# Float32 tables and row-half counts in the subset look-up of a four-layer graph network

## The chip, the cores and the metric

The kernel runs on one core of one Trainium2 chip. The metric is the device time of one execution in microseconds (us), lower is better. Before the change the median of three runs is 6579.31 us, and the three lie between 6573.1 and 6581.36 us.

## The reference, cut to what matters

Sixteen graphs of N = 1024 nodes with 128 features pass four layers, each followed by a residual and a normalisation. The adjacency matrix of a graph holds only zeros and ones. The change touches layer 1 alone:

```
p = x @ (W1 - W2);  q = x @ W2
pre[i, j] = p[i] + q[j] + b
x1[i] = max over j of relu(pre[i, j]) * adj[i, j]
```

As relu is monotone, this is `relu(p[i] + b + max of q[j] over the neighbours j of i)`. The costly part is the maximum over neighbours, for 1024 nodes, 1024 possible neighbours and 128 features in each of 16 graphs.

The other layers matter as work that runs beside it: layer 0 is masked attention, layer 2 a two-layer perceptron on summed neighbours, and layer 3 three graph convolutions on a thinned ("dilated") adjacency matrix, which is found by a sequential pass over its rows.

## The kernel before, in words

**The maximum as a table look-up.** The 1024 possible neighbours of a graph are cut into `NP` = 86 groups of 12, and a group into two subgroups of `GS` = 6. A subgroup has 64 subsets, and for each subset the maximum of q over it is worked out once: two subgroups give a table of 128 rows. For a node i, the part of its adjacency row that falls on a subgroup names one subset. So the maximum over a subgroup is one row of the table, and a matrix product of the table with a one-hot column picks it out.

**One slot** handles one group s of one graph b; there are 16 x 86 = 1376 slots, and each has two halves h of 512 nodes (`halves[h]`). The loop `slot(s, last)` writes out the order of the instructions of TensorE (PE), ScalarE (ACT), VectorE (DVE) and GpSimd (POOL) by hand, and each of these engines runs its list in that order. In a half stand, in this order:

1. `look_up(s, h, pg)` (L779): four products on TensorE. A product uses 64 of the 128 rows, since a subgroup's table has 64 rows: rows 0 to 63 for subgroup a = 0, rows 64 to 127 for a = 1, into two banks of the PSUM tile `pg` (two buffers of two banks). The table is held in two pieces, `high` and `low`, both of type float32r, whose products add up in PSUM.
2. `advance(...)`: pieces of the other work, taken from generators called streams (`scores`, `attend`, `rest`, `tables_of`) by a planner that gives each engine so many microseconds of other work in each slot (`ROOM`). At a due time it also takes a piece of `dilation()`, the sequential pass for layer 3, whose chain runs on GpSimd and VectorE.
3. `low_part(s + 1)` in the first half of odd slots (L768, L770): TensorE subtracts `high` from the table in PSUM by a product with `less` (minus the identity), and ScalarE copies the rest out as `low`.
4. `count(s + 2, h)` (L748, L749): one product of the constant `lit` (plus and minus ones) with the adjacency columns `AT`, 120 rows in fp8, counts for each of the 128 subsets how well each node matches it; ScalarE then forms `relu(count + one_less)`, which is the one-hot `hot`. It runs two slots ahead of the look-up.
5. `table(s + 2)` in the second half of even slots (L760, L763): TensorE transposes two groups' subset maxima `sub` into the tile `pt`, and ScalarE copies that out as `high`.
6. VectorE takes the running maximum `best = max(best, pg)` over both subgroups, 1024 values in each partition (L831).

The tiles `pm` of `count` and `pt` of `table` share a tag, "subset", of two one-bank buffers in PSUM; `pt` is kept until `low_part` is done. The adjacency columns come by `load_columns` (L700), one DMA on GpSimd's queue for 120 rows (ten slots), two loads ahead, in four buffers.

When the slots are done, the graph convolutions of layer 3 follow in a stage of their own, which has none of this code.

Of the kernel before, what the change touches and what calls it, by code (L numbers as in the profile page):

```python
# [39 lines left out]
B, N, D, H2 = 16, 1024, 128, 256  # L40
P = 128
T = N // P
GS = 6
PS = 2 * GS
PC = 10
CH = PC * PS
NP = -(-N // PS)
TG = 12
R, G = 32, 4
# [9 lines left out]
def subset_tables():  # L59

    half = P // 2
    s = np.arange(half)
    lit = np.zeros((CH, PC, P), np.float32)
    for j in range(CH):
        a, k = divmod(j % PS, GS)
        lit[j, j // PS, a * half:(a + 1) * half] = np.where((s >> k) & 1, 1.0, -1.0)
    size = sum((s >> k) & 1 for k in range(GS))
    return lit, np.tile(1.0 - size, 2).astype(np.float32).reshape(P, 1)


@with_exitstack
def tile_graph_layers(ctx: ExitStack, tc, a, out):
    nc = tc.nc
    x, adj, adjT = a["x"], a["adj"], a["adjT"]
    halves = (slice(0, 512), slice(512, 1024))

    consts = ctx.enter_context(tc.tile_pool(name="consts", bufs=1))
    dram = ctx.enter_context(tc.tile_pool(name="dram", bufs=1, space=DRAM))
    small = ctx.enter_context(tc.tile_pool(name="small", bufs=3))
    psum = None  # L80
# [9 lines left out]
    psum = setup.enter_context(tc.tile_pool(name="psum0", bufs=2, space=PSUM))  # L90
    ident = consts.tile([P, P], F32, name="ident")
# [13 lines left out]
    less = consts.tile([P, P], F32R, name="less")  # L105
    nc.vector.tensor_scalar_mul(less, ident, -1.0)
    one_less = consts.tile([P, 1], F32, name="one_less")
    nc.sync.dma_start(out=one_less, in_=a["one_less"])
# [52 lines left out]
    pm = bank("pm")  # L161
# [74 lines left out]
    def layers_012():  # L236
# [4 lines left out]
        apool = es.enter_context(tc.tile_pool(name="apool", bufs=1))  # L241
# [451 lines left out]
        def load_columns(at):  # L693
            b, c = divmod(at, T + 1)
            if b < B:
                rows = min(CH, N - c * CH)
                t = AT[at] = apool.tile([CH, N], F8, name="AT", bufs=4)
                if rows < CH:
                    nc.gpsimd.memset(t, 0.0)
                nc.gpsimd.dma_start(out=t[:rows], in_=adjT[b, c * CH:c * CH + rows])  # L700

        An, AT, subs, qs, ps, values, exps, bests, hots, tables = ({} for _ in range(10))
        now, taken, given, held = 0, 0, {}, {}
        pending = {}
# [33 lines left out]
                        given[held[stream]] = now + 0.5  # L738
                    pending[stream] = [next(stream, None), now]

        def count(s, h):

            b, g = divmod(s, NP)
            c, r = divmod(g, PC)
            if h == 0:
                hots[s] = w2.tile([P, N], F32R, name="hot", bufs=3)
            pm = psum.tile([P, 512], F32, tag="subset", name="pm", bufs=2)
            nc.tensor.matmul(pm, lit[:, r, :], AT[b * (T + 1) + c][:, halves[h]], start=True, stop=True)  # L748
            nc.scalar.activation(hots[s][:, halves[h]], pm, AF.Relu, bias=one_less)  # L749

        def table(s):

            b, g = divmod(s, NP)
            g0 = g - g % TG
            assert ("sub", b, g0) in happened, (s, [(x.__name__, pending[x]) for x in streams], room)
            pt = psum.tile([P, 512], F32, tag="subset", name="pt", bufs=2)[:, :2 * P]
            if g + 2 - g0 == min(TG, NP - g0):
                happened["used", b, g0] = now
            for k in range(2):
                nc.tensor.matmul(pt[:, k * P:(k + 1) * P], subs[b, g0][:, g - g0 + k, :], ident, is_transpose=True,  # L760
                                 start=(k == 0), stop=(k == 1))
            high = w2.tile([P, 2 * P], F32R, name="high", bufs=2)
            nc.scalar.copy(high, pt)  # L763
            tables[s] = pt, high

        def low_part(s):
            pt, high = tables[s]
            nc.tensor.matmul(pt, less, high, start=False, stop=True, skip_group_check=True)  # L768
            low = w2.tile([P, 2 * P], F32R, name="low", bufs=2)
            nc.scalar.copy(low, pt)  # L770
            tables[s] = high, low

        def look_up(s, h, pg):

            at = s % 2
            for k, part in enumerate(tables[s - at]):
                for a in range(2):
                    rows = slice(64 * a, 64 * a + 64)
                    nc.tensor.matmul(pg[:, a], part[rows, at * P:(at + 1) * P], hots[s][rows, halves[h]],  # L779
                                     start=(k == 0), stop=(k == 1))  # L780

        def finish(b):

# [7 lines left out]
        def slot(s, last):  # L791

            nonlocal now, due, wants_bank
            now = s
            b, g = divmod(s, NP)
            if s >= 0 and g == 0:
                finish(b)
                if b + 1 < B:
                    start(tables_of(b + 1), True)
                    load_x(b + 1)  # L800
                    start(attend(b + 1))
                    start(scores(b + 1))
                if b:
                    start(rest(b - 1))
            if s >= 0 and g % PC == 0:
                load_columns(b * (T + 1) + g // PC + 2)
            for h in range(2):
                now = s + 0.5 * h
                for e in ROOM:
                    room[e] = min(room[e] + ROOM[e] / 2, ROOM[e])  # L810
                if s >= 0:
                    pg = psum.tile([P, 2, 512], F32, tag="wide", name="pg", bufs=2)
                    look_up(s, h, pg)
                advance(("PE",))
                advance(("A", "V", "Pool"))
                if s >= 0 and due <= now and not (wants_bank and taken >= 2 and given.get(taken - 2, 1e9) > now):
                    after, cost, wants_bank = next(dilate, (B * NP, 0, False))
                    due += after
                    room["V"] -= cost
                if h == 0 and s % 2 and s + 1 < last:  # L820
                    low_part(s + 1)
                if s + 2 < last:
                    count(s + 2, h)
                    if h and s % 2 == 0:
                        table(s + 2)
                if s >= 0:
                    own = bests[b][:, :, halves[h]]
                    if g == 0:
                        nc.vector.tensor_copy(own, pg)
                    else:  # L830
                        nc.vector.tensor_max(own, own, pg)  # L831
            if s >= 0:
                hots.pop(s)
# [341 lines left out]
```

## Time and profile before

| What | Value |
|---|---|
| median of 3 runs | 6579.31 us |
| span of the profiled execution | 6568.2 us |
| the profiled execution's own time | not among the times shown; the median lies 11.1 us above its span |
| slot stage, first to last look-up | 131 to 5279 us, 5148 us, 3.74 us a slot |
| stage of layer 3 after it | 5279 to 6568 us, 1289 us |
| VectorE busy in the slot stage | 4704.24 us |
| TensorE busy in the slot stage | 4529.59 us |
| ScalarE busy in the slot stage | 3168.41 us |
| GpSimd busy in the slot stage | 3563.30 us |

The profile is of one execution. Busy time is the time in which an engine has an instruction in flight. [...]records of neighbouring matmuls overlap: what a matmul costs the engine is the distance from its start to the start of the next, where nothing else holds that up. A float32 product of TensorE has two records (two passes), a float32r product one.

### The profile page before, as it was taken

The page shows a single profiled execution, that of the slowest core. Times are in us where ns is not written, and L with a number is a line of the kernel's source. Part 1 is how long each engine was busy: PE and PEld are TensorE (multiplying, and loading weights), DVE is VectorE, ACT ScalarE, POOL GpSimd, SP SyncE. Part 2 cuts the span into 40 slices and gives each one's busy share as a digit, 9 for nine tenths or more (in the row PEclk, how much of TensorE's full clock was granted, in tenths as well). Part 3 has the DMA queues.
Part 4 walks back from the last instruction along what each step waited for, and adds up shares of the span by engine and source line. Part 5 has one row for each costly group of instructions (what it writes and reads, how often), then busy time and mean ns, then how long its engine had stood idle before and what let it go on. Part 6 is the DMA issues. An engine that isn't in the chain of part 4 may idle for free. (4 is left out here: it accounts for less than half of the span.)

```text
span 6568.2 us, 85836 instructions
## 1 busy us (share of the span) xinstructions
PE 5661.4 (86%) x27177; PEld 2873.0 (44%) x27306; DVE 5317.8 (81%) x8130; ACT 3780.8 (58%) x6665; POOL 3794.2 (58%) x11157
## 2 busy tenths in 40 slices
PE   6989898989898989899989898888888768877998
PEld 3434344444343444444444444444443335555654
DVE  3999899999899999999999999999998844444445
ACT  4656566666666666666666666666665533333755
POOL 2675767676767776767677776767676611110113
PEclk8989899999898989898989998999898878888999
DMA  5121212121212121212121212121110056564555
GB/s 38 13 28 23 31 23 36 21 28 26 28 26 29 24 30 27 27 27 28 26 27 27 30 26 33 23 31 27 27 26 12 14 80 125 110 119 106 199 170 183
DMA packets 478380, 317.00 MB, mean 48 GB/s; under 512 B 301162, under 2 KB 429668, under 8 KB 473828
## 3 DMA queue, kind: packets, MB, share of 16 engines
q0 software_dynamic: 105648, 84.20, 14.9%
q1 hardware_dynamic: 367600, 226.13, 11.9%
q8 instruction: 213, 3.49, 0.2%
q10 hardware_dynamic: 4676, 1.19, 0.1%
q14 instruction: 243, 1.99, 0.1%
HBM read 412.71 MB, written 117.18 MB: 81 GB/s over the span
## 5 line engine op out<-in xcount | busy, mean ns | idle before, releaser
L831 DVE TENSOR_TENSOR best<-best,pg 128x1024 f32<-128x1024 f32 x2720 | 3234.4, 1211 | 298.4 <-PE pg L779 289.4
L749 ACT ACTIVATE hot<-pm,one_less 128x512 fp32r<-128x512 f32 x2752 | 1882.1, 688 | 1118.0 <-PE pm L748 1107.3
L779 PE MATMUL pg<-hot,high 64*128 64x512 f32 x5504 | 1471.9, 532 | 468.0 <-DVE best L831 426.2
L779 PE MATMUL pg<-hot,low 64*128 64x512 f32 x5504 | 1166.7, 420 | 0.0
L748 PE MATMUL pm<-AT,lit 120*128 120x512 fp8e4 x2752 | 1135.9, 413 | 17.9 <-ACT hot L749 10.1
L779 PEld LDWEIGHTS pg<-hot,high 64*128 64x128 f32 x5504 | 545.7, 195 | 1271.7 <-DVE best L831 801.5
L616 POOL TENSOR_SCALAR sc<-low_counts,half_mask,rest 16x1 f32<-16x1 f32 x992 | 426.5, 430 | 403.9 <-DVE rest L603 310.1
L779 PEld LDWEIGHTS pg<-hot,low 64*128 64x128 f32 x5504 | 570.2, 204 | 0.0
L748 PEld LDWEIGHTS <-lit 120*128 120x128 fp8e4 x2752 | 273.7, 99 | 618.7 <-issue 556.1
L621 POOL TENSOR_SCALAR sc<-sc 16x1 f32<-16x1 f32 x992 | 425.5, 429 | 105.0
L770 ACT CAST low<-pt 128x256 fp32r<-128x256 f32 x688 | 255.5, 371 | 393.7 <-PE pt L768 389.3
L618 POOL TENSOR_SCALAR sc<-sc 16x1 f32<-16x1 f32 x992 | 351.6, 354 | 107.7
L980 POOL TENSOR_TENSOR length<-length,mhalf 128x8 f32<-128x8 f32 x48 | 78.9, 1644 | 572.2 <-DVE length L979 572.2
L624 POOL TENSOR_SCALAR last_rank<-V,sc 16x31 f32<-16x31 bf16 (+30 forms) x992 | 384.7, 388 | 0.0
L623 POOL TENSOR_SCALAR hit<-V,sc 16x31 bf16<-16x31 bf16 (+30 forms) x992 | 372.7, 376 | 0.0
L768 PE MATMUL pt<-high,less 128*128 128x256 f32 x688 | 300.9, 437 | 66.3 <-ACT high L763 58.7
L467 DVE TENSOR_TENSOR sub<-sub,q 128x24 f32<-128x24 f32 (+11 forms) x768 | 306.5, 400 | 24.6 <-ACT q L289 10.5
L937 ACT CAST m<-near 128x1024 fp32r<-128x1024 fp8e4 x256 | 253.4, 1044 | 113.1 <-DVE near L906 59.4
L619 POOL TENSOR_SCALAR sc<-sc 16x1 f32<-16x1 f32 x992 | 269.9, 272 | 83.4
L760 PE MATMUL pt<-ident,sub 128*128 128x128 f32 x1376 | 292.8, 297 | 24.5 <-ACT hot L749 22.0
L626 POOL TENSOR_TENSOR low_counts<-low_counts,hit 16x31 f32<-16x31 f32 (+30 forms) x992 | 264.6, 267 | 77.7
L377 PE MATMUL pav<-v,eT 128*128 128x128 f32 x2048 | 307.6, 296 | 1.9 <-ACT eT L370 1.9
(258 smaller groups left out, 9431.7 us busy)
## 6 DMA issues: line engine op xcount, KB each, us to landing
removed<-gone SPq DMA_DIRECT2D x128, 256.0 KB
An<-in_adj_dram POOLq DMA_DIRECT2D x16, 1024.0 KB, 14.8
E<-in_adj_dram POOLq DMA_DIRECT2D x128, 128.0 KB, 6.8
gone_all<-removed POOLq DMA_DIRECT2D x64, 256.0 KB, 12.1
near<-in_adjT_dram POOLq DMA_DIRECT2D x16, 1024.0 KB, 17.3
kept<-near SPq DMA_DIRECT2D x16, 1024.0 KB
share<-share SPq DMA_DIRECT2D x32, 512.0 KB
hidden<-r SPq DMA_DIRECT2D x32, 512.0 KB
```

The source lines that it names most:

```text
L377: nc.tensor.matmul(pav, eT[:, c, :], values[b][:, c, :], start=(c == 0), stop=(c == T - 1))
L467: nc.vector.tensor_max(sub[:, :n_g, n:2 * n], sub[:, :n_g, 0:n], qg[:, 2 * g0:2 * g0 + n_g, k:k + 1].to_broadcast([P, n_g, n]))
L616: gp.tensor_scalar(half, mine, half_mask[:, m], rest[:, n:n + 1], op0=ALU.mult, op1=ALU.add)
L618: gp.tensor_scalar(sf, half, 5.5, sf, op0=ALU.is_gt, op1=ALU.mult)
L621: gp.tensor_scalar(to, at, sf, none, op0=ALU.subtract, op1=ALU.subtract)
L623: gp.tensor_scalar(hit[:, n, n + 1:], V[:, n, n + 1:], at, None, op0=ALU.is_equal)
L624: gp.tensor_scalar(last[:, n + 1:], V[:, n, n + 1:], to, None, op0=ALU.is_le)
L748: nc.tensor.matmul(pm, lit[:, r, :], AT[b * (T + 1) + c][:, halves[h]], start=True, stop=True)
L749: nc.scalar.activation(hots[s][:, halves[h]], pm, AF.Relu, bias=one_less)
L768: nc.tensor.matmul(pt, less, high, start=False, stop=True, skip_group_check=True)
L779: nc.tensor.matmul(pg[:, a], part[rows, at * P:(at + 1) * P], hots[s][rows, halves[h]], start=(k == 0), stop=(k == 1))
L831: nc.vector.tensor_max(own, own, pg)
```

## The change

The table is kept in one float32 piece instead of two float32r pieces; `low_part`, `less` and the copy `low` are gone, and a look-up has two float32 products instead of four float32r ones. The counts of both node halves are made at once, in the first half of a slot: the adjacency columns lie in bf16, nodes 0 to 511 in partitions 0 to 59 and nodes 512 to 1023 in partitions 64 to 123, and a 61st row of ones (partitions 60 and 124) adds the bias that came from `one_less`. The two products of 61 rows go into the two banks of one tile `pm`, and one activation over 1024 columns makes `hot`. The tag "subset" now has one buffer of two banks, which `pm` and `pt` take in turn. The columns lie in three fixed tiles, set to one at the start, and are loaded by two DMAs (four for a graph's last, short chunk). The program has 320 such DMAs in place of 144.

```diff
-        for j in range(CH):
+        for j in range(SUB):                      # SUB = CH // 2 = 60
-    lit = consts.tile([CH, PC, P], F8, name="lit")
+    lit = consts.tile([P, PC // 2, P], BF, name="lit")
...
-                t = AT[at] = apool.tile([CH, N], F8, name="AT", bufs=4)
-                if rows < CH:
-                    nc.gpsimd.memset(t, 0.0)
-                nc.gpsimd.dma_start(out=t[:rows], in_=adjT[b, c * CH:c * CH + rows])
+                t = AT[at] = columns_in[at % len(columns_in)]
+                for part, s in enumerate(halves):
+                    whole = rows // SUB
+                    first = c * CH + whole * SUB
+                    nc.gpsimd.dma_start(out=t[64 * part:64 * part + SUB, :whole],
+                                        in_=adjT[b, c * CH:first, s].rearrange("(j r) m -> r j m", r=SUB))
+                    if rows % SUB:
+                        nc.gpsimd.dma_start(out=t[64 * part:64 * part + rows % SUB, whole],
+                                            in_=adjT[b, first:first + rows % SUB, s])
...
+        columns_in = [apool.tile([P, 2, 512], BF, name=f"AT{i}") for i in range(3)]
+        for t in columns_in:
+            nc.vector.memset(t, 1.0)
...
-        def count(s, h):
+        def count(s):
...
-            if h == 0:
-                hots[s] = w2.tile([P, N], F32R, name="hot", bufs=3)
-            pm = psum.tile([P, 512], F32, tag="subset", name="pm", bufs=2)
-            nc.tensor.matmul(pm, lit[:, r, :], AT[b * (T + 1) + c][:, halves[h]], start=True, stop=True)
-            nc.scalar.activation(hots[s][:, halves[h]], pm, AF.Relu, bias=one_less)
+            j, r = divmod(r, PC // 2)
+            hots[s] = w2.tile([P, N], F32, name="hot", bufs=3)
+            pm = psum.tile([P, 2, 512], F32, tag="subset", name="pm", bufs=1)
+            for part in range(2):
+                rows = slice(64 * part, 64 * part + SUB + 1)
+                nc.tensor.matmul(pm[:, part], lit[rows, r, :], AT[b * (T + 1) + c][rows, j, :], start=True, stop=True)
+            nc.scalar.activation(hots[s], pm.rearrange("p h n -> p (h n)"), AF.Relu)
...
-            pt = psum.tile([P, 512], F32, tag="subset", name="pt", bufs=2)[:, :2 * P]
+            pt = psum.tile([P, 2, 512], F32, tag="subset", name="pt", bufs=1)[:, 0, :2 * P]
...
-            high = w2.tile([P, 2 * P], F32R, name="high", bufs=2)
-            nc.scalar.copy(high, pt)
-            tables[s] = pt, high
-        def low_part(s):
-            pt, high = tables[s]
-            nc.tensor.matmul(pt, less, high, start=False, stop=True, skip_group_check=True)
-            low = w2.tile([P, 2 * P], F32R, name="low", bufs=2)
-            nc.scalar.copy(low, pt)
-            tables[s] = high, low
+            tables[s] = w2.tile([P, 2 * P], F32, name="table", bufs=2)
+            nc.scalar.copy(tables[s], pt)
...
-            for k, part in enumerate(tables[s - at]):
-                for a in range(2):
-                    rows = slice(64 * a, 64 * a + 64)
-                    nc.tensor.matmul(pg[:, a], part[rows, at * P:(at + 1) * P], hots[s][rows, halves[h]],
-                                     start=(k == 0), stop=(k == 1))
+            for a in range(2):
+                rows = slice(64 * a, 64 * a + 64)
+                nc.tensor.matmul(pg[:, a], tables[s - at][rows, at * P:(at + 1) * P], hots[s][rows, halves[h]],
+                                 start=True, stop=True)
...
-                if h == 0 and s % 2 and s + 1 < last:
-                    low_part(s + 1)
                 if s + 2 < last:
-                    count(s + 2, h)
-                    if h and s % 2 == 0:
+                    if h == 0:
+                        count(s + 2)
+                    elif s % 2 == 0:
                         table(s + 2)
```

More of the change, by code (lines that the diff above doesn't have):

```diff
@@ L46 @@
 CH = PC * PS
+SUB = CH // 2
 NP = -(-N // PS)
@@ L62, in subset_tables @@
     s = np.arange(half)
-    lit = np.zeros((CH, PC, P), np.float32)
-    for j in range(CH):
+    lit = np.zeros((2, half, PC // 2, P), np.float32)
+    for j in range(SUB):
         a, k = divmod(j % PS, GS)
-        lit[j, j // PS, a * half:(a + 1) * half] = np.where((s >> k) & 1, 1.0, -1.0)
+        lit[:, j, j // PS, a * half:(a + 1) * half] = np.where((s >> k) & 1, 1.0, -1.0)
     size = sum((s >> k) & 1 for k in range(GS))
-    return lit, np.tile(1.0 - size, 2).astype(np.float32).reshape(P, 1)
+    return lit.reshape(P, PC // 2, P), np.tile(1.0 - size, (PC // 2, 2)).astype(np.float32)
 @with_exitstack
@@ L102, in tile_graph_layers @@
     nc.vector.memset(mhalf, -0.5)
-    lit = consts.tile([CH, PC, P], F8, name="lit")
+    lit = consts.tile([P, PC // 2, P], BF, name="lit")
     nc.gpsimd.dma_start(out=lit, in_=a["lit"])
[L105 to L108, printed above, removed]
+    for part in range(2):
+        nc.gpsimd.dma_start(out=lit[64 * part + SUB:64 * part + SUB + 1],
+                            in_=a["one_less"].rearrange("(o r) m -> o r m", o=1))
     def weight(name, shape=(P, P), how=None, pool=consts):
@@ L739, in advance @@
                     pending[stream] = [next(stream, None), now]
[L741 removed]
+        def count(s):
             b, g = divmod(s, NP)
             c, r = divmod(g, PC)
[L745 to L749 removed]
+            j, r = divmod(r, PC // 2)
+            hots[s] = w2.tile([P, N], F32, name="hot", bufs=3)
+            pm = psum.tile([P, 2, 512], F32, tag="subset", name="pm", bufs=1)
+            for part in range(2):
+                rows = slice(64 * part, 64 * part + SUB + 1)
+                nc.tensor.matmul(pm[:, part], lit[rows, r, :], AT[b * (T + 1) + c][rows, j, :], start=True, stop=True)
+            nc.scalar.activation(hots[s], pm.rearrange("p h n -> p (h n)"), AF.Relu)
         def table(s):
```

## The prediction, made before the changed kernel was run

> **What bounds the kernel now.** I read the page's slices first, to see where time passes.
>
> ```profile
> PE   6989898989898989899989898888888768877998
> DVE  3999899999899999999999999999998844444445
> PEclk8989899999898989898989998999898878888999
> ```
>
> In 31 of the 40 slices VectorE is at 8 or 9 tenths, and TensorE with it. That is the slot stage; the windows put numbers on it.
>
> ```profile
> 131.00:5279.00 5148.00, 4529.59 (x22015) 2168.15 (x22141) 4704.24 (x6944) 3168.41 (x5820) 3563.30 (x10742) 0.91 0.19 26
> 5279.00:6568.00 1289.00, 1056.40 (x4860) 655.25 (x4858) 581.07 (x1067) 570.15 (x778) 202.42 (x358) 0.90 0.56 138
> ```
>
> After length come PE, weight loads, DVE, ACT and POOL busy, then clock. VectorE works 4704 of 5148 us (91%), TensorE's records cover 4530; ScalarE and GpSimd have room. The groups and waits tell which of the two waits for which.
>
> ```profile
> L831 DVE TENSOR_TENSOR best<-best,pg 128x1024 f32<-128x1024 f32 x2720 | 3234.4, 1211 | 298.4 <-PE pg L779 289.4
> L779 PE MATMUL pg<-hot,high 64*128 64x512 f32 x5504 | 1471.9, 532 | 468.0 <-DVE best L831 426.2
> ...
> L748 PE MATMUL pm<-AT,lit 120*128 120x512 fp8e4 x2752 | 1135.9, 413 | 17.9 <-ACT hot L749 10.1
> ```
> ```profile
> PEld pg L779 <- DVE best L831: 801.5, 1213, 13.1
> ```
>
> The look-up waits for VectorE to empty `pg` more (426 us of idle matmul time, 802 us at its weight loads) than VectorE waits for it (289). So VectorE is the tighter one, TensorE close behind. What TensorE's work costs unhindered I take from the timeline, start to start:
>
> ```profile
> 1501.71 0.40 PE L779 MATMUL pg<-hot,low 64*128 64x512 f32 x2
> 1502.04 1.12 PE L329 MATMUL psc<-kT,qT 128*128 128x512 f32 x2
> 1503.21 0.60 PE L278 MATMUL ptr<-ident,X 128*128 128x128 f32 x4
> ...
> 2503.11 0.38 PE L748 MATMUL pm<-AT,lit 120*128 120x512 fp8e4 x1
> 2503.33 0.38 PE L760 MATMUL pt<-ident,sub 128*128 128x128 f32 x2
> 2503.65 0.50 PE L779 MATMUL pg<-hot,high 64*128 64x512 f32 x2
> 2503.98 0.40 PE L779 MATMUL pg<-hot,low 64*128 64x512 f32 x2
> ```
> ```profile
> 2504.53 0.38 PE L768 MATMUL pt<-high,less 128*128 128x256 f32 x1 [0.16 <-ACT high L763]
> 2504.76 0.39 PE L748 MATMUL pm<-AT,lit 120*128 120x512 fp8e4 x1
> 2505.08 0.50 PE L779 MATMUL pg<-hot,high 64*128 64x512 f32 x2
> ```
>
> The x2 of L779 is a pair on the two row halves, and both run in the time of one. `high` to `low` is 0.33 us, `low` to the next group 0.33, a count before a look-up 0.32, before a transpose 0.22, a transpose pair 0.32, `low_part` 0.23. The float32 score product (two passes, and 0.22 for a penalty product whose record is missing) takes 1.17.
>
> **What the Trainium skill says.** "FP8 and Floating Point Precision", TensorE Precision Notes: float32 needs four passes, reduced float32 one. The trace agrees: the float32 records of L329 are two for a product, median 593 ns each, against 390 for float32r at L950 with the same 512 columns; the difference, 0.20 us, is another 512 columns. "TensorE: Matmul & The Clock Gate", Part 3: row tiles overlap, but matmuls start and end in order, and only weight loads are pulled ahead. The pair of L779 agrees on the overlap; that a second float32 product overlaps only the last pass of the first is not shown by any record. "TensorEngine Tiling (Array Packing)", Key Properties: a change of tiling mode drains the engine. The trace agrees: L779 after L748 starts after 0.32 us, L760 after L748 after 0.22, so a drain costs 0.10. "ScalarE: Activation LUTs", What ACT_TABLE_LOAD costs: a pointer operand adds about 93 ns to an activation; here 687 ns (L749, with one) against 597 (L315, without).
>
> **The change part by part, in TensorE time of the slot stage.** *Before:* look-ups 2752 x 0.67 = 1844; counts 2065 x 0.32 + 687 x 0.22 = 812; transposes 687 x 0.32 = 220; `low_part` 687 x 0.23 = 158; other streams, their own starts added up, 1128. Sum 4162, against VectorE's 4704. The stage took 5148, which is 1.094 times the larger.
>
> *Look-ups after.* A float32 pass streams for 1.17 - 0.22 - 0.10 (first weight load) = 0.85 for two, so 0.43. The order on the queue is first half pass 1, pass 2, second half pass 1, pass 2. As matmuls start in order, the second half's pass 1 can run beside the first half's pass 2 at best: three steps of 0.43, not two. In the changed program's instruction order, look-ups and counts form 1634 unbroken stretches of row-half work (495 a look-up alone, 492 a count and a look-up, 293 look-up, count, look-up, the rest longer). Stepped through by that rule, they have 7895 pass steps: 7895 x 0.427 = 3371. Each stretch has a first weight load and a drain, 0.207: 338. *Counts:* a pair costs one 0.22, and lies beside a last pass except in the 613 at the head of a stretch: 135. So look-ups and counts cost 3844 instead of 2656, **+1188**. *Removed:* `low_part`, -158, and with it waits for its copy (58 us idle matmul time, 238 at weight loads), which are in no sum of needs. *Transposes* stay, with drains and shared starts 254, +34. *Streams:* 1284 blocks now meet row-half work at their end too, 0.10 each, +128. New sum 3844 + 254 + 1256 = **5354**.
>
> *VectorE* is unchanged, 4704; three memsets come at the start. So **TensorE becomes the bound**. *ScalarE:* 1376 activations at about 1.04 (L943, 1024 columns without pointer) replace 2752 at 0.687, -460, and `low` goes, -256. It was not the bound: 0.
>
> *The wait that is added.* `pm` and `pt` now take turns in one buffer. On even slots the transposes wait until `hot` is done: 0.38 record + 0.04 + 1.04 = 1.46 after the count; one look-up and its drain (0.22 + 1.39) lie between, so 0.15 is spare. Behind the waiting transposes stands all of TensorE, and then VectorE, which waits for `pg`. A stream's activation ahead of `hot` (0.59 to 1.15) eats the spare; 349 of 687 transposes follow the look-up directly. Cost from 0 to 349 x 1 = 350; I take 100. The next count waits for the table copy (0.37), behind a look-up of 1.39: 0, up to 100 if activations stand ahead of it.
>
> *GpSimd's queue:* 176 more DMA issues at 0.66 (L700) = +117, less 16 memsets of 0.94. They stand in the dilation's chain, which has a third of the stage idle: 0; without that cover 100. With three buffers a load waits for counts three slots back, and has some ten slots (over 37 us) to land, against 29.6 at most: 0. *Start:* two small DMAs more on POOL's queue before the mask rows, one fewer on SP's, the memsets: 0, bounds -1 and +4. *Stage after:* none of this code, 0.
>
> **The sum.** A stage whose bound is 5354, with VectorE at 88% of that instead of TensorE, has fewer coinciding peaks than before, and fuller TensorE windows should raise the clock from 0.91; the buffer wait goes the other way. I take 1.08 (bounds 1.02 and 1.13, where 1.094 was before): 5354 x 1.08 = 5782, +634. On the profiled execution that is 6568.2 + 634 = 7202; the median is 11 us above its span: **7213 us**.
>
> **The rivals.** *Passes of the row halves don't overlap at all:* 5504 products x 0.854 = 4700, + 338 + 302 (counts) + 254 + 1256 = 6850, nearly alone: x 1.03 = 7055, +1907, **8490**. For it: no float32 record in 64 rows exists yet; against it: nothing in the float32r pair hints at a bar. *Passes pair up perfectly* (two steps): 2350 + 338 + 302 + 254 + 1256 = 4500, still under VectorE; the stage gains some waits: about 5250, **6680**. Against it: matmuls start in order. *Faster:* **a 64-row float32 pass streams one column a clock**, 0.213: 7895 x 0.213 = 1682, + 338 + 135 + 254 + 1256 = 3665. TensorE then waits for VectorE, and the stage sinks to 4704 x 1.045 = 4915, -233: **6346**. It decides from a pass of (4162 - 1983) / 7895 = 0.276 us downwards. Against it: L329's 593 ns. *Not doing what it says* (halves not split over row groups) is the first rival.
>
> **The numbers.** What a measurement of this kernel can tell from no change is about 0.2%. Forecast 0.60, no overlap 0.20, perfect pairs 0.08, faster 0.10, no change 0.02. Faster 0.10, same 0.02, slower 0.88. The range takes in the forecast (its floor, 5354 x 1.02 and no waits, is 6900, less some for the step count) and the first rival: 6800 to 8500.
>
> **What would show it.** Right: two float32 records of L780 about 0.43 apart in each half, three steps a look-up, 1.3 to 1.5 us from its start to the next group; TensorE busy over 93% of the stage; VectorE's `best` waiting for `pg` several times 289 us; `pg` waiting for `best` near nothing; clock above 0.95; the stage of layer 3 at 1289. Wrong: a look-up of 0.9 or of 1.8 us, a transpose waiting for `hot` by several hundred us, or VectorE still the engine that is waited for.

## The result, and the profile after

The changed kernel takes **6694.93 us** (median of 4 runs, 6688.31 to 6696.37), against 6578.89 us for the kernel before on the same chip (4 runs, 6573.1 to 6581.36): 116 us more, a ratio of 1.0174 with a 95% interval of 1.016 to 1.0188. The sign of the forecast was right. The size was not: 7213 was forecast, and the measurement lies 105 us under the low end of the range. The rival "passes pair up perfectly", with 6680, came within 15 us and had a chance of 0.08.

The profiled execution has a span of 6693.7 us. Its slices, in tenths of 40 equal parts:

```profile
PE   6989898989898989898989898989897868787998
DVE  3899899899989999999998989888898844444445
PEclk8999999999999999999999999999998988888999
```

Both engines look as they did, but PEclk is 9 almost throughout the slot stage, where the kernel before alternates between 8 and 9. The windows (length, busy PE, weight loads, DVE, ACT and POOL, then clock) put it in numbers.

```profile
131.00:5400.00 5269.00, 4693.10 (x21310) 1882.17 (x21430) 4726.82 (x6939) 2613.91 (x3756) 3680.71 (x10899) 0.97 0.19 28
5400.00:6693.00 1293.00, 1062.49 (x4872) 657.98 (x4872) 585.28 (x1071) 571.72 (x779) 202.85 (x358) 0.90 0.56 138
```

The first window ends at 5400 us; the last look-up starts at 5405.2. From first to last look-up the slot stage took 5276 us for 5148, and layer 3's stage after it 1288.5 for 1289, so the whole loss is in the slot stage. VectorE's work is what it was (4727 for 4704). TensorE's records cover only 164 us more than before (4693 for 4530), not the thousand and more that a need of 5354 would show. The clock rose from 0.91 to 0.97.

The groups of the slot stage follow. After the count of instructions come busy time, mean ns of one, the idle time of the engine just before them, and what ended most of that. The two lines after them are weight loads: what they waited for, us in all, how often, and the longest.

```profile
L831 DVE TENSOR_TENSOR best<-best,pg 128x1024 f32<-128x1024 f32 x2720 | 3248.6, 1213 | 438.0 <-PE pg L780 416.5
L780 PE MATMUL pg<-hot,table 64*128 64x512 f32 x11008 | 3063.2, 637 | 417.6 <-DVE best L831 380.1
L759 ACT ACTIVATE hot<-pm 128x1024 f32<-128x1024 f32 x1376 | 1407.8, 1023 | 1633.3 <-PE pm L758 1627.1
L758 PE MATMUL pm<-AT,lit 61*128 61x512 bf16 x2752 | 541.4, 388 | 11.9 <-ACT table L773 2.9
L770 PE MATMUL pt<-ident,sub 128*128 128x128 f32 x1376 | 291.3, 294 | 108.9 <-ACT hot L759 106.9
```
```profile
PEld pg L780 <- DVE best L831: 953.6, 1027, 12.5
PEld pt L770 <- ACT hot L759: 399.0, 390, 12.0
```

Read the last columns of the groups first. `best` waits for `pg` 417 us, where it was 289: these 127 us more of VectorE's idle time are about the loss of the stage (128). But `pg` still waits for `best` too, 380 us (before, 426), and its weight loads 954 us (before, 802). An engine that had become the sole bound would not be kept waiting so by the other. The two are now level. The last line is the wait that the change adds, transposes for `hot`: 107 us of idle matmul time, and 399 us at their weight loads. It replaces smaller ones: in the kernel before, the transposes waited 22 us for `hot`, and `low_part` 59 us (239 at its weight loads) for its copy.

The timeline shows what a float32 look-up costs:

```profile
2500.78 0.38 PE L758 MATMUL pm<-AT,lit 61*128 61x512 bf16 x2
2501.00 1.02 PE L780 MATMUL pg<-hot,table 64*128 64x512 f32 x4
2502.34 0.44 PE L770 MATMUL pt<-ident,sub 128*128 128x128 f32 x2 [0.32 <-ACT hot L759]
2502.71 1.13 PE L780 MATMUL pg<-hot,table 64*128 64x512 f32 x4
2503.77 1.13 PE L329 MATMUL psc<-kT,qT 128*128 128x512 f32 x2
2505.04 0.39 PE L758 MATMUL pm<-AT,lit 61*128 61x512 bf16 x2
```

The count pair costs 0.22, from 2500.78 to 2501.00. The look-up at 2502.71 hands over to the next group at 2503.77, after 1.06 us; where its first weight load lies under other work it is 0.95. Its x4 are two passes on each of two row halves. The score product at 2503.77, whose two passes use all 128 rows, has a record of the same length: the two halves cost no more than one. The single records in the trace begin at 2502.711 and 2502.718 (pass 1 of the halves) and at 3.244 and 3.251 (pass 2). That is two steps, not three.

### The profile page after: what moved, and what is told of

It reads as the page before. It is cut to its first block, busy times and chain, and to the rows that moved or that the text cites. A ratio compares the mean times of both kernels' runs of the same rounds, so it can differ in the third digit from the quotient of the medians.

```text
span 6693.7 us, 83260 instructions
## 1 busy us (share of the span) xinstructions
PE 5831.7 (87%) x26493; PEld 2589.8 (39%) x26618; DVE 5347.9 (80%) x8132; ACT 3228.3 (48%) x4601; POOL 3915.7 (58%) x11319
## 5 line engine op out<-in xcount | busy, mean ns | idle before, releaser
L780 PE MATMUL pg<-hot,table 64*128 64x512 f32 x11008 | 3063.2, 637 | 417.6 <-DVE best L831 380.1
L759 ACT ACTIVATE hot<-pm 128x1024 f32<-128x1024 f32 x1376 | 1407.8, 1023 | 1633.3 <-PE pm L758 1627.1
L780 PEld LDWEIGHTS pg<-hot,table 64*128 64x128 f32 x11008 | 939.8, 191 | 1328.2 <-DVE best L831 953.6
L758 PE MATMUL pm<-AT,lit 61*128 61x512 bf16 x2752 | 541.4, 388 | 11.9 <-ACT table L773 2.9
L621 POOL TENSOR_SCALAR sc<-sc 16x1 f32<-16x1 f32 x992 | 436.2, 440 | 104.2
L773 ACT COPY table<-pt 128x256 f32<-128x256 f32 x688 | 255.3, 371 | 405.6 <-PE pt L770 400.6
L618 POOL TENSOR_SCALAR sc<-sc 16x1 f32<-16x1 f32 x992 | 351.3, 354 | 107.4
L770 PEld LDWEIGHTS pt<-ident,sub 128*128 128x128 f32 x1376 | 160.1, 143 | 469.1 <-ACT hot L759 399.0
L377 PEld LDWEIGHTS pav<-v,eT 128*128 128x128 f32 x2048 | 256.1, 197 | 186.7 <-issue 126.6
L619 POOL TENSOR_SCALAR sc<-sc 16x1 f32<-16x1 f32 x992 | 275.7, 278 | 83.2
L758 PEld LDWEIGHTS <-lit 61*128 61x128 bf16 x2752 | 142.5, 94 | 440.1 <-issue 421.6
L625 POOL TENSOR_TENSOR hit<-hit,last_rank 16x31 bf16<-16x31 bf16 (+30 forms) x992 | 252.7, 255 | 82.6
L617 POOL TENSOR_SCALAR sc<-sc 16x1 f32<-16x1 f32 x992 | 249.5, 251 | 86.8
```

Source lines behind the costliest of these rows:

```text
L377: nc.tensor.matmul(pav, eT[:, c, :], values[b][:, c, :], start=(c == 0), stop=(c == T - 1))
L618: gp.tensor_scalar(sf, half, 5.5, sf, op0=ALU.is_gt, op1=ALU.mult)
L621: gp.tensor_scalar(to, at, sf, none, op0=ALU.subtract, op1=ALU.subtract)
L758: nc.tensor.matmul(pm[:, part], lit[rows, r, :], AT[b * (T + 1) + c][rows, j, :], start=True, stop=True)
L759: nc.scalar.activation(hots[s], pm.rearrange("p h n -> p (h n)"), AF.Relu)
L780: nc.tensor.matmul(pg[:, a], tables[s - at][rows, at * P:(at + 1) * P], hots[s][rows, halves[h]], start=True, stop=True)
```

## The experiments

All ratios are to the kernel before on the same chip, with 95% intervals. The edits are against the changed kernel unless said otherwise.

### Do the row halves wait for each other?

A kernel of TensorE products alone (the network is left out), in groups between blocks of full bf16 products, at full clock throughout. Its queue holds the lower half's products first, then the upper half's:

```diff
+for rows, bank in ((low, 0), (low, 1), (high, 4), (high, 5)):      # L52
+for rows, bank in ((low, 0), (low, 1), (low, 2), (low, 3),
+                   (high, 4), (high, 5), (high, 4), (high, 5)):     # L57
```

> A kernel that only measures products on TensorE (the network is left out). After a warm-up, ten times each: two float32 products of 512 columns, one on rows 0-63 and one on rows 64-127; two on the lower rows and then two on the upper; four and four; two on the lower rows alone; two and two in float32r; two on all 128 rows. Each group is closed by four full bf16 products. Theory Order (matmuls start in the order of the queue, as the prediction had it): the pair has three steps of 0.43 us, 1.28 in all; two and two have seven steps, 3.0; four and four fifteen. Theory Overtake (a product on the other row half starts as soon as its own rows are free): the pair has two steps, 0.85; two and two four steps, 1.71; four and four eight, 3.4, if the look-ahead reaches so far. Two on the lower rows alone are four steps, 1.71, in both.

Its timeline: one product on each half (L45, L47), two on each half (L52), four on each half (L57), and two on the lower half alone (L62).

```profile
18.52 0.69 PE L45 MATMUL bank<-x 64*128 64x512 f32 x1
18.52 0.69 PE L47 MATMUL bank<-x 64*128 64x512 f32 x1
19.05 0.59 PE L45 MATMUL bank<-x 64*128 64x512 f32 x1
19.06 0.59 PE L47 MATMUL bank<-x 64*128 64x512 f32 x1
...
38.80 1.99 PE L52 MATMUL bank<-x 64*128 64x512 f32 x8
40.73 1.04 PE L35 MATMUL bank<-xb 128*128 128x512 bf16 x4
...
67.74 5.52 PE L57 MATMUL bank<-x 64*128 64x512 f32 x16
73.19 1.04 PE L35 MATMUL bank<-xb 128*128 128x512 bf16 x4
...
149.25 1.98 PE L62 MATMUL bank<-x 64*128 64x512 f32 x4
```

Pass 1 of both halves begins at 18.52, pass 2 of both at 19.05. Two products on each half (1.99) take as long as two on one half alone (1.98): four steps for eight passes. Records do not name the half, but two passes of one half lie 0.429 us apart (L62), so passes that start together are on different halves. In single records the upper half's first pass starts 0.013 us after the lower's, though four passes stand ahead of it on the queue; the first step is 0.533 and the others are 0.429. In float32r the same queue takes two steps of 0.33. With four products on each half the upper half starts only after 1.83 us, when four lower passes have run, and the group takes 5.45 us to the next start. That is twelve steps of 0.43, where perfect pairing needs eight and strict order fifteen. So a product for idle rows overtakes earlier ones, and in these two cases the reach is about four passes. In a look-up the second product has two passes ahead of it and pairs up fully. Of the two theories Overtake held, except for its eight steps with four products on each half. This settles the failed step.

### The table alone

The kernel before with `hot` and the table in float32 and without `low_part`, its counts and activations left as they were:

```diff
...
-            tables[s] = high, low
+            tables[s] = w2.tile([P, 2 * P], F32, name="table", bufs=2)
...
```

> The kernel before with the float32 table alone: low_part and its copy gone, look-ups in float32, counts as they were. Theory Need (TensorE's own time decides): 4162 - 158 + 2752 x 0.39 (a look-up of 1.06 in place of 0.67) = about 5080 us of need, over VectorE's 4704: stage 5300 to 5500, total 6730 to 6930, slower than the whole change. Theory Wait (the cost comes from the one-buffer ring of counts and transposes): the two-buffer ring stands here, so no wait of the transposes for hot; total 6550 to 6610.

6926.22 us, ratio 1.0526 (1.051 to 1.0542), **347 us more** than before. Its slot stage, and the groups:

```profile
129.70:5643.90 5514.20, 5209.07 (x21455) 1941.62 (x21454) 4781.71 (x6950) 2987.99 (x5133) 3576.00 (x10742) 0.98 0.17 24
```
```profile
L820 DVE TENSOR_TENSOR best<-best,pg 128x1024 f32<-128x1024 f32 x2720 | 3285.7, 1214 | 621.1 <-PE pg L770 612.1
L770 PE MATMUL pg<-hot,table 64*128 64x512 f32 x11008 | 3169.3, 653 | 254.0 <-DVE best L820 226.9
```

The time is inside Theory Need's range, and the stage 14 us above it. This is what TensorE as the bound looks like: busy 94% of the stage, `best` waiting 612 us for it, and it waiting only 227 us for `best` (406 us at weight loads, for 954 in the changed kernel). So much of the forecast's picture came true in this version, with full 120-row counts between float32 look-ups. The counts on row halves, with what comes with them, take it away again: the changed kernel is 231 us faster than this one.

### The wait for `hot`

Two ways. First, the transposes moved to the start of even slots:

```diff
+                if h == 0 and s % 2 == 0 and s + 2 < last:
+                    table(s + 2)
...
-                    elif s % 2 == 0:
-                        table(s + 2)
```

> The changed kernel with the transposes of the table moved from the second half of even slots to their start, ahead of the look-up, so that they no longer follow the count of their own slot in the one-buffer ring. Theory Need: the wait for hot (107 us of idle matmul time, 399 at the weight loads) goes, but TensorE's need of 4450 stays: 6620 to 6680. Theory Wait: the cost of the change is this wait, and it goes: 6580 or less.

6703.02 us, ratio 1.0186 (1.017 to 1.0201). This is outside both ranges. The wait hardly shrank (89.5 us, 269 times, for 107 and 284). The edit was a bad test: at the new place there is again just one look-up between the previous count and the transposes. VectorE's idle time ahead of `best` only moved along, from the first halves of odd slots (167 us, now 72) to those of even slots (83, now 206). The run says nothing about what the wait costs.

Second, two one-bank tiles and two activations, so that the ring has two buffers again:

```diff
-            pm = psum.tile([P, 2, 512], F32, tag="subset", name="pm", bufs=1)
+            pms = [psum.tile([P, 512], F32, tag="subset", name="pm", bufs=2) for part in range(2)]
...
-            nc.scalar.activation(hots[s], pm.rearrange("p h n -> p (h n)"), AF.Relu)
+            for part, pm in enumerate(pms):
+                nc.scalar.activation(hots[s][:, halves[part]], pm, AF.Relu)
```

> The changed kernel with its last part undone: the counts of the two halves go into two one-bank tiles, each with an activation of 512 columns, and counts and transposes share two one-bank buffers again. The transposes then wait for the first, shorter activation alone (0.38 + 0.04 + 0.60 = 1.02 after the count, in place of 1.46), which a look-up of 0.96 and a drain cover. Theory Need (TensorE's greater need, in slots where it exceeds VectorE's work, is the whole cost): the 107 us of idle matmul time before the transposes go, and what is saved is at most that; 6630 to 6690. Theory Wait (that wait sets the cost): 6580 or less. Nothing or slower would say that the wait lies beside others.

6639.92 us, ratio 1.0112 (1.0091 to 1.0133). The group of the transposes:

```profile
L771 PE MATMUL pt<-ident,sub 128*128 128x128 f32 x1376 | 289.2, 292 | 20.1 <-ACT hot L760 18.2
```

The wait falls from 107 to 18 us (from 399 to 280 at weight loads), and the ratio by 0.0062, which is 41 us, within the range of Theory Need. So the single tile with its single activation costs about 41 us, give or take 17. By the trace it does so by delaying the look-up behind the transposes: VectorE's idle time ahead of `best` falls by 68 us in all, 55 of them in the first halves of odd slots, right behind the transposes.

### Less work on TensorE, and filler

The table and `hot` in one reduced piece (float32r), so that a look-up has one pass in each half; the table's low piece is left out.

```diff
-            hots[s] = w2.tile([P, N], F32, name="hot", bufs=3)
+            hots[s] = w2.tile([P, N], F32R, name="hot", bufs=3)
...
-            tables[s] = w2.tile([P, 2 * P], F32, name="table", bufs=2)
+            tables[s] = w2.tile([P, 2 * P], F32R, name="table", bufs=2)
```

> The changed kernel with table and one-hot in float32r in a single piece: one pass for each look-up product in place of two. It leaves out the low part of the table, so the picked values are rounded. Theory Need: TensorE's need falls by 2752 x 0.427 = 1175 to about 3275; the stage sinks towards VectorE's 4704, to 4850 to 5000: total 6270 to 6430. Theory Wait: the transposes wait for hot as before, and longer, since the look-up that lies between is shorter: 6600 to 6700.

6478.81 us, ratio 0.9848 (0.9831 to 0.9864). The look-ups lose about 2752 x 0.43 = 1180 us of TensorE time, and the kernel only 216; its time lies between the two ranges. Its slices and its slot stage:

```profile
PEclk8868697868686968787878777777776578888999
```
```profile
128.60:5181.30 5052.70, 3767.79 (x15952) 1757.86 (x15951) 4676.50 (x6950) 2610.94 (x3758) 3697.88 (x10899) 0.77 0.19 29
```

The granted clock of the stage is down to 0.77, and VectorE, at 4677 of 5053 us, is the bound. Then the same kernel with every count product given out three times, about 600 us of filler on TensorE:

```diff
-            for part in range(2):
+            for part in (0, 1) * 3:
```

> The kernel with the table in one float32r piece (its low part left out) and every count product issued three times over, with the same result: about 0.44 us more TensorE work in a slot, 600 in all, to no purpose. It stands beside the run with one piece, 6479 at a granted clock of 0.794. Theory Need in its plain form: more work for TensorE can only cost, 6480 to 6600. Theory Clock (idle stretches of TensorE halve its clock, and so give back what smaller need saves): the clock rises to 0.9 or more, and the time stays or falls: 6400 to 6480.

6492.16 us, ratio 0.9886 (0.9863 to 0.9909). The filler costs about 0.4% (0.9848 to 0.9886), and the two intervals touch: inside Theory Need's range in its plain form, and outside Theory Clock's. The clock of the stage rises to 0.86, short of the 0.9 expected. The added work went two ways. TensorE's idle time in the stage fell from 1285 us (5053 - 3768) to 1056 (5070 - 4014), and with the higher clock its other work got shorter: a record of the score product has a mean of 740 ns without the filler and 674 with it (646 in the changed kernel). So while VectorE is the bound, work added to TensorE goes into its idle time and is in part paid for by a higher clock, and work taken away leaves idle time and a lower clock. No run tells the two shares apart.

### Less work on VectorE

`best` over 256 of each half's 512 nodes (the others are left out), in the kernel before and in the changed one:

```diff
-                        nc.vector.tensor_max(own, own, pg)
+                        nc.vector.tensor_max(own[:, :, :256], own[:, :, :256], pg[:, :, :256])
```

> The kernel before with VectorE taking the running maximum over 256 of each 512 nodes (the other half is left out), 0.53 us less for each of 2752 instructions: VectorE's need falls to about 3250, so that TensorE's own floor shows. Theory Need: the stage comes to TensorE's sum of 4162 over a clock of 0.95 to 0.98 and some waits: 4350 to 4600, total 5780 to 6030.

> The changed kernel with the same cut of VectorE's maximum (half of the nodes left out). Theory Need: TensorE's floor is about 290 us higher than in the kernel before, 4450 in place of 4162, over a clock near 1: the difference of the two cut kernels is 200 to 350. Theory Wait: the difference is larger than the need explains, 400 or more, as the wait of the transposes for hot stands on the chain too.

6367.13 and 6473.93 us (one run each). The first is 194 us under the kernel before on that chip (6561.14), the second about 201 us under 1.0174 times that. The first is far above its range, and the difference of the two, 107 us, is under both ranges of the second. The slot stage of the first, up to 5000 us:

```profile
131.00:5000.00 4869.00, 4355.98 (x21768) 2102.70 (x21891) 3324.07 (x6869) 3121.29 (x5754) 3534.18 (x10622) 0.93 0.20 27
```

The stage ends at 5076 us. In its 4946 us VectorE is busy 3370 us (68%), 1334 less than before, and still the kernel gained only a seventh of that. So VectorE was never the only thing that holds the stage at 5148: TensorE (4356 of 4869 us) stands just behind, and perhaps something else. The dilation's chain is a candidate: VectorE's wait for its DMA `hit_p` rises from 62 to 183 us, and GpSimd's own part of a step, 128 us, does not shrink. The length of a step (160.2 us in the kernel before, 154.1 here) says nothing, since the program gives out the chain's pieces by slots and a step spans about 43 slots in both. No run took the chain away, so a third floor is not shown. The gap between the two kernels stays, 107 us for 116.

### The loads of adjacency columns

The kernel before with each load in two DMAs, 288 for 144; and the changed kernel with 15 slots a load, 224 for 320; and the latter with two activations besides.

```diff
-                nc.gpsimd.dma_start(out=t[:rows], in_=adjT[b, c * CH:c * CH + rows])
+                for s in halves:
+                    nc.gpsimd.dma_start(out=t[:rows, s], in_=adjT[b, c * CH:c * CH + rows, s])
```
```diff
-        columns_in = [apool.tile([P, 2, 512], BF, name=f"AT{i}") for i in range(3)]
+        columns_in = [apool.tile([P, 3, 512], BF, name=f"AT{i}") for i in range(2)]
...
-            if s >= 0 and g % PC == 0:
+            if s >= 0 and g % 15 == 0:
```

> The kernel before with every load of adjacency columns issued as two DMAs of 512 columns: 288 issues on GpSimd's queue in place of 144, nothing else changed. Theory Queue (the issues stand in the sequential chain of the dilation on GpSimd, and that chain sets the pace of the slot stage with the others): 144 x 0.66 = 95 us on the chain; the time rises by 50 to 95, to 1.008 to 1.014 of the kernel before. Theory Tensor (TensorE's greater need in the slots is the whole cost of the change, GpSimd has cover): ratio 0.998 to 1.003.

> The changed kernel with longer loads of adjacency columns: 180 nodes (15 slots) in a load in place of 120, in two tiles of three parts in place of three of two; 224 DMA issues in place of 320 on GpSimd's queue. Theory Queue: 96 x 0.68 = 65 us less on GpSimd's chain; the time falls by 35 to 65, to a ratio of 1.007 to 1.012 to the kernel before, against 1.017 for the change. Theory Tensor: 1.016 to 1.019, as the change.

> The changed kernel with both: longer loads, and the two activations of 512 columns in two one-bank buffers (which stood at 1.011 to the kernel before). If the wait of the transposes and GpSimd's queue are separate costs, the gains add up: 1.011 - 0.006 to 0.010 = 1.001 to 1.005. If they are the same stretches of time seen twice, 1.008 to 1.011.

1.0038 (1.0024 to 1.0052), 1.0187 (1.0173 to 1.0201) and 1.0099 (1.0085 to 1.0113). Adding 144 DMAs to the kernel before costs 25 us. The first ratio lies between the two ranges expected for it, the second in Theory Tensor's range, and the third in the second of its two. Taking 96 from the changed one gains nothing that can be measured, with one activation or with two. So nothing shows that the 116 us went into DMA issues, though the cost in the kernel before is not nothing; no run took away all 176 that the change adds, and why they cost there and not here stays open.

One wait on that queue the prediction had excluded. In the changed kernel GpSimd's loads wait 113.1 us, 27 times and up to 26.9 us, for counts of the tile that they overwrite; in the kernel before they wait 4.5 us for counts. To take it away, each load is given out four slots later:

```diff
-            if s >= 0 and g % PC == 0:
+            if s >= 0 and g % PC == 4:
```

> The changed kernel with each load of adjacency columns given out four slots later (at the fifth slot of ten, so that the counts of the tile that it overwrites lie seven slots back; it still comes 14 slots ahead of its first count). Theory Load wait: in the changed kernel GpSimd's loads wait 113 us, 27 times, for counts of the tile that they overwrite, and the dilation's chain stands behind them on the queue; without that the kernel is 15 to 60 us faster, ratio to the kernel before 1.008 to 1.015. Theory Idle: GpSimd only waits there because it has run ahead of the slots and would wait at its next step anyway; the wait shrinks below 30 us, another of GpSimd's waits grows by as much, and the ratio stays between 1.016 and 1.019.

1.0179 (1.0166 to 1.0193), where the changed kernel has 1.0174. Two of GpSimd's waits in this run:

```profile
POOL counts L504 <- DVE start_at L666: 320.8, 27, 19.8
...
POOL AT L701 <- PE pm L758: 47.7, 17, 26.7
```

The loads' wait falls from 113 to 48 us (below 30 was expected), and another wait on that queue, of the dilation's tile `counts` for `start_at`, rises from 236 to 321. GpSimd had only run ahead: it waits at another place instead. The same edit in three other versions:

> The same later loads in the version with two tiles of one bank and two activations a slot, which took 1.0112 of the kernel before. Load wait: 1.002 to 1.009. Idle: 1.009 to 1.013.

> The same later loads in the version that counts on row halves with the table in two reduced pieces, which took 1.0015 of the kernel before and whose loads wait 76 us. Load wait: 0.992 to 0.999. Idle: 1.000 to 1.003.

> The same later loads in the version with one reduced piece (the table's low piece is left out), which took 0.9848 of the kernel before and whose loads wait 54 us. Load wait: 0.976 to 0.983. Idle: 0.983 to 0.987.

1.0109 (1.0094 to 1.0125), 1.001 (1.0004 to 1.0017) and 0.9851 (0.9838 to 0.9865), against 1.0112, 1.0015 and 0.9848 without it. All four are in the ranges of Theory Idle: the edit moves nothing that can be measured.

### Counts on row halves with two pieces

The kernel before with the new counts, two activations, and its two reduced pieces of the table, so that only the float32 table is undone. The low piece has its own transposes, since `pt` is no longer kept, and the node mask lies in one byte in SBUF to make room (that part of the edit is not shown):

```diff
+            high = w2.tile([P, 2 * P], F32R, name="high", bufs=2)
+            nc.scalar.copy(high, pt)
...
+        def low_part(s):
+            pt = psum.tile([P, 512], F32, tag="subset", name="pt", bufs=2)[:, :2 * P]
...
+            nc.tensor.matmul(pt, less, high, start=False, stop=True, skip_group_check=True)
```

> A version of its own: counts on the row halves as in the change, in two one-bank tiles with two activations, but the table in two float32r pieces as before; the low piece transposes the subset maxima a second time instead of keeping the bank, just behind the look-up in the first half of odd slots. (The node mask lies in one byte in SBUF to make room.) TensorE's need is about 3650 (look-ups 2752 x 0.43 of streaming instead of 0.85). Theory Tensor: the stage goes to about 5050 as with the single piece: ratio 0.980 to 0.992 to the kernel before. Theory Queue: its 320 DMA issues keep GpSimd's chain long, and a clock at 0.8 gives TensorE's gain back: 0.990 to 1.000.

6576.2 us, ratio 1.0015 (1.0009 to 1.0022), with a mean clock of 0.905 over the whole run. It is as fast as the kernel before, within 10 us, and not faster; both theories expected 1.000 or less. So the cheaper counts gain nothing that can be seen in this version. Whether they would alone is not shown: it also transposes the subset maxima a second time and has 320 loads for 144, and 144 more loads cost the kernel before 25 us. Its first look-up starts at 138.2 us, for 131.3 before, so about 7 of the 10 us lie ahead of the slots.

With this run the 116 us come apart into parts. The new counts with two activations and two pieces, second transposes and byte mask included: 0.15%, 10 us. The float32 table in their place (1.0015 to 1.0112): 64 us. One tile and one activation for two (1.0112 to 1.0174): 41 us. They add up to the whole by construction, so the sum is no check. These are differences of ratios from different groups of runs; the last two are uncertain by about 15 us each.

Of the versions that take the maximum over all nodes, only the ones with a single reduced piece beat the kernel before. They do so by keeping less of the table, so they do another computation; no version with the table kept in full did.

## Why the prediction was right or wrong

**The failed step is "three steps of 0.43, not two".** It took from the Trainium skill, "TensorE: Matmul & The Clock Gate", Part 3, that matmuls start and end strictly in the order of issue. Here the measurement decides against that for products on different row tiles: in the probe the upper half starts 0.013 us after the lower, ahead of passes that were issued before it. The same goes for the sentence ahead of the prediction that each engine runs its list in the order written: on TensorE it does not hold across row halves. The prediction itself noted that no record before showed the overlap of a second float32 product, and then took the stricter rule as its likeliest case. The price of a pass was right (0.43 forecast, 0.429 measured), and so was the count pair (0.22). Its own sign for being wrong, a look-up of 0.9 us, is what came (0.95).

**The mis-sized term is "look-ups after".** With two steps in place of three its 3371 becomes 2350, and the counts get 302 for 135. The sum of TensorE's needs is then the perfect-pairs rival's 4500, not 5354. The trace bears it out. An estimate of the need adds up, for each pair of neighbouring kinds of groups, the lower quartile of their start-to-start distances: 4520 to 4630 for the changed kernel's stage, by how the records are grouped, and about 4220 for before, where the prediction had 4162. TensorE's need rose by some 300 to 410 us, not by 1192.

**"TensorE becomes the bound" fell with it.** 4500 lies under VectorE's 4704. That the sign came out all the same is no support for this step: the kernel is slower, but not because TensorE alone sets its time. The signs named for it failed: TensorE is busy 89% of the stage (over 93% forecast); `best` waits for `pg` 1.4 times as long (several times forecast); `pg` waits for `best` 380 us (near nothing forecast). The version with the float32 table alone shows that the signs themselves were good ones: it has the first (94%) and goes part of the way on the others (612 us, 2.1 times as long, and 227 us). The factor of 1.08 over TensorE's need fits there: the same lower quartiles give 5111, and 5111 x 1.08 = 5520 for a stage of 5514.

**The cost of two level bounds.** In the changed kernel the stage is 1.12 times VectorE's 4704, for 1.094 before: with TensorE closer behind, VectorE waits for it more often (697 times for 555). The perfect-pairs rival took 1.116 (5250 / 4704) for this and was near. Its two steps were the mechanism; its factor had no working behind it, so that it came within 15 us is in part luck.

**The clock** was called in sign (above 0.95 in the stage; 0.97 measured), but its size was not put into the sum. A rough estimate: 4162 / 0.91 = 4574 us of real time before and 4500 / 0.97 = 4639 after, so that of 338 us of added need about 65 are left. An average clock is no account of single waits, and no run shows that the loss came about in this way.

**Right:** the ring wait was given 0 to 350 with 100 taken, and costs about 41 together with the single activation. The activation was priced at 1.04 and took 1.023; ScalarE is not the bound, since the version with two activations gives it more work and is faster. GpSimd's added DMA issues were put at 0, and 96 fewer of the 176 indeed give nothing. Layer 3's stage was put at 1289 (1288.5). **Right in cost, wrong in mechanism:** "three buffers, 0". The load does wait (113 us), and it costs nothing because GpSimd runs ahead of the slots, not because the counts are done.

**Open:** what holds the stage at 4946 us when VectorE has a third less to do; why 144 more DMAs cost 25 us in the kernel before while 96 fewer give nothing in the changed one; and what the wait for `hot` costs by itself, since the run that nearly removes it also splits the activation.

## What to carry to other kernels

Before a rule about order decides a forecast, measure it: a short kernel of bare products showed in one run what the trace of the kernel before could not, and the rule was worth 500 us. When an engine that is not the bound gains or loses work, expect most of it to vanish into idle time and into the granted clock; 1180 us taken from TensorE were worth 216, and 600 us added cost about 0.4%. And take a large change apart: each half of this one, the table (+347) and the counts (-231 on top of it, +10 in the version that kept two pieces), had another worth beside the other than by itself.

## What was not expected of the hardware

- A product on one row half overtakes earlier products of the other half: float32 products queued lower, lower, upper, upper take four steps of 0.429 us. The look-ahead ends after about four passes in this probe: with four products on each half the upper starts at 1.83 us, and the group takes twelve steps.
- A 64-row float32 product has two passes of 0.43 us for 512 columns, as one of 128 rows does (probe records 0.429 apart in both). A bf16 product of 512 columns is 0.216 apart here, and four of those are the 0.86 of a float32 product, which fits the four passes that the prediction cites.
- The granted clock falls on partly busy stretches too. The Trainium skill, "TensorE: Matmul & The Clock Gate", Part 1, puts the half clock after an idle window of about 3.4 us. In these traces the granted clock is either 1.0 or 0.5. In the kernel before, the 3.4 us ahead of a fall to 0.5 had TensorE busy for about half of the time (median 0.47; 0.37 in the changed kernel, 0.51 in the one-piece version), so partly idle windows suffice here. In the one-piece version TensorE's records cover 75% of the stage and the mean clock is 0.77; in the changed kernel they cover 89%, and it is 0.97. The share alone does not set it: the kernel before has 88% and 0.91.
